# Two layers of routed experts: 33 slots of whole and quartered expert rows in place of 34 of whole and halved ones

## The chip, the cores and the metric

One core of a Trainium2 chip runs the whole program. The metric is the device time of one execution in microseconds (us). Engines are named as in the profile: PE is TensorE's matmuls, PEld its weight loads, DVE is VectorE, ACT is ScalarE, POOL is GpSimd, SP is SyncE. Rows are gathered and scattered by indirect DMAs that POOL issues.

## The reference

x has 8 x 256 = 2048 tokens of 512 values. Two layers follow each other, and each adds a routed feed-forward part to x. Cut to what matters here:

```python
# layer 0: each token takes two of 8 experts; an expert is a 512x512 matrix made from atoms
logits = clip(xt @ gate_w.T, -50, 50)
top_w, top_idx = top_k(logits, 2)
rw = softmax(top_w)
...                      # out = xt @ W.T + sum over the two of rw * (xt @ delta[expert])
x = x + layer0(...)      # xt is the attention's output

# layer 1
probs = softmax(x1 @ gate_w)
gate_score, gate_idx = top_k(probs, 2)
combine = onehot weights * alpha
h = gelu(x1 @ fc1_w[e] + fc1_b[e])
y = h @ fc2_w[e] + fc2_b[e]
out = sum over e of y[e] * combine[:, e]
```

So each layer has 2 x 2048 = 4096 pairs of token and expert, 512 for each expert on average. With the given inputs the experts hold 542, 416, 510, 556, 504, 526, 508 and 534 pairs in layer 0, and 542, 526, 490, 492, 520, 543, 510 and 473 in layer 1.

## The kernel before

**Slots.** A layer's pairs are laid into slots of 128 rows, 34 in each layer. A slot gathers its 128 token rows from DRAM (`fetched`, L682, an indirect DMA by POOL), turns them on PE (`turned`, L718 and L724, tile `pa`), multiplies them by an expert's weights (`multiplied`), scales each row by its routing weight and adds the rows to the result in DRAM by an accumulating indirect DMA (`added`, L729, POOL again).

**Plan.** `Plan` (L53) fixes at build time which expert a slot serves. *Full* slots serve one fixed expert; the first eight take the first 128 rows of each expert and only tokens of the first tiles, so that they can start early. The rest are *side* slots of two halves: the upper 64 rows go to a fixed expert (`plan.side`), the lower 64 to an expert that the routing finds at run time (`owners` reads it into registers). Layer 0 has 16 full and 18 side slots, layer 1 has 22 and 12. An expert's rows go in order of their rank to its first slot, its side halves, its further full slots and then to run-time halves. Rows that find no place are marked in `left`; if there are any, `run_rest` (L2095) routes and runs them in a slow branch. A token whose two rows fall into one slot is sent there too (`twice`, L514), because one accumulating DMA must not name a row twice.

**Routing.** `route` (L456) works out the slot and the row of each pair with a few dozen small DVE operations on 128 x 128 and 128 x 32 tiles, and `fill_slots` turns them into lists of tokens and weights with matmuls on one-hot tiles. `routing_constants` makes the plan's steps with iotas on POOL (L195).

**multiplied (L692).** A full slot runs four matmuls of 512 columns, one for each chunk of 128 of the contraction (the profile counts two instructions for each fp32 matmul). A side slot runs eight, on two column halves of the array in turn (L705), each half with its own 64 rows as the stationary operand and its own expert's weights as the moving one.

**slots0 (L1988)** is layer 0: one multiplication a slot, ACT scales the rows (L2029), and the adds of slot s go to one of two DRAM tensors, `sums_d[s % 2]`, which are added together later (`read`, L2152, loads `part` by SP at L2158). Weights of layer 1 are loaded meanwhile, one expert with each of the slots 8 to 23 (`load_first`, `load_second`).

**Between the layers** the adapters and the gate are folded on PE, `x1` is read, turned (L2165) and multiplied by the gate (`inner`, tile `px`, L2172, four column quarters), routed, and multiplied by the layer's matrix (`outer`, L2204), which fills PE until about 655 us.

**slots1 (L2263)** is layer 1. A full slot multiplies in turned form at once (L2299, tile `pu`); a side slot makes `ph`, copies it and turns it back (L718). ACT applies Gelu with the expert's bias, one instruction for each chunk and expert of the slot (L2325). The second multiplication gives `py`; DVE adds the second bias, once for each expert of the slot (L2341), and scales the rows (L2343). All adds go to `out`. The loop runs the first multiplication of slot s, then the second of slot s - 1, then Gelu of slot s, and turns the rows of slot s + 2; gathers run three or more slots ahead.

The program's order on the engines is fixed at build time. Before an add, POOL waits on semaphores for its input and for earlier adds to the same tensor.

Of the kernel before, what the change touches and what calls it, by code (L numbers as in the profile page):

```python
# [11 lines left out]
F32 = mybir.dt.float32  # L12
I32 = mybir.dt.int32
# [16 lines left out]
SCALE = 256.0**-0.5  # L30
EPS = 1e-6
E = 8
HR = P // 2
NREST = 2 * N // P + E - 1
NS = 4096
NSC = NS // P
# [16 lines left out]
class Plan:  # L53
# [5 lines left out]

    PAIRED, FULL = 128 * HR, 256 * HR

    def __init__(self, full, side, tiles):
        self.full = list(range(E)) + [e for e in range(E) for _ in range(full[e] - 1)]
        self.side = [e for e in range(E) for _ in range(side[e])]
        self.tiles = tiles
        self.F, self.D = len(self.full), len(self.side)
        self.n = self.F + self.D
        self.by_expert = []  # L70
        for e in range(E):
            t = P + HR * side[e]
            u = t + P * (full[e] - 1)
            early = self.FULL + P * e
            second = self.PAIRED + HR * (self.F + sum(side[:e])) - P
            whole = self.FULL + P * (E + sum(full[:e]) - e) - t
            first = HR * self.F - u
            self.by_expert.append((t, u, early + 1, second - early, whole - second, first - whole))


PLAN0 = Plan([2] * E, [2] * 6 + [3] * 2, 8)
PLAN1 = Plan([3] * 6 + [2] * 2, [1] * 6 + [3] * 2, 12)


@with_exitstack
def two_layer_kernel(ctx: ExitStack, tc: tile.TileContext, io: dict, out: bass.AP):
# [369 lines left out]
    def route(keep, pool, psum, consts, plan, sel, coef, tag, beside=None, skip=0, quads=False):  # L456
# [4 lines left out]
        pn, prk = ranks(pool, psum, consts, sel)  # L461
        have = pool.tile([P, E], F32, name="have")
        nc.vector.tensor_tensor(have, pn, fixed[:, 1, :], ALU.subtract)
        boff, bend = units(pool, keep, tag, consts, have, HR)
        nc.vector.scalar_tensor_tensor(
            boff, boff, float(HR), fixed[:, 5, :], ALU.mult, ALU.add
        )
        each = [P, NT, E]
        row = keep.tile(each, F32, name=f"row_{tag}")
# [23 lines left out]
        nc.vector.tensor_scalar(  # L493
            at_i, rows.rearrange("p r i -> p (r i)"), 1.0, None, ALU.subtract
        )
        is_full = pool.tile(both, F32, name="is_full")
        nc.vector.tensor_scalar(is_full, at_i, float(plan.FULL), None, ALU.is_ge)
        shift_i = pool.tile(both, I32, name="shift_i")
        nc.vector.tensor_scalar(shift_i, is_full, 6.0, None, ALU.add)
        mask_i = pool.tile(both, I32, name="mask_i")  # L500
        nc.vector.tensor_scalar(mask_i, is_full, float(HR), float(HR - 1), ALU.mult, ALU.add)
        second = pool.tile(both, F32, name="second")
        nc.vector.tensor_scalar(second, at_i, float(plan.PAIRED), None, ALU.is_ge)
        nc.vector.tensor_tensor(second, second, is_full, ALU.subtract)
        nc.vector.tensor_tensor(mask_i, at_i, mask_i, ALU.bitwise_and)
        rem = pool.tile(both, F32, name="rem")
        nc.vector.scalar_tensor_tensor(rem, second, float(HR), mask_i, ALU.mult, ALU.add)
        nc.vector.tensor_tensor(at_i, at_i, shift_i, ALU.arith_shift_right)
        nc.vector.tensor_scalar(at_i, at_i, 127, None, ALU.bitwise_and)
        slot = pool.tile(both, F32, name="slot")  # L510
        nc.vector.tensor_copy(slot, at_i)

        twice = pool.tile([P, NT], F32, name="twice")
        nc.vector.tensor_tensor(twice, slot[:, :NT], slot[:, NT:], ALU.is_equal)  # L514
        nc.vector.scalar_tensor_tensor(
            slot[:, :NT], twice, 128.0, slot[:, :NT], ALU.mult, ALU.add
        )
# [174 lines left out]
    def multiplied(py, xT, weights, experts):  # L692

        if len(experts) == 1:
            for k in range(KC):
                nc.tensor.matmul(  # L696
                    py,
                    xT[:, k, :],
                    of_expert(experts[0])(weights(k)),
                    start=(k == 0),  # L700
                    stop=(k == KC - 1),
                )
            return
        in_a_row(
            lambda k=k, h=h: nc.tensor.matmul(  # L705
                py[h * HR : (h + 1) * HR, :],
                xT[:, k, h * HR : (h + 1) * HR],
                of_expert(experts[h])(weights(k)),
                start=(k == 0),
                stop=(k == KC - 1),  # L710
            )
            for k in range(KC)
            for h in (1, 0)
        )

    def transposed(dst, src):
# [3 lines left out]
    def turned(pool, psum, xs, copy=nc.vector.tensor_copy):  # L720
        pa = psum.tile([P, KC, P], F32, name="pa")
        transposed(pa, xs)
        xsT = pool.tile([P, KC, P], F32, name="xsT")
        copy(xsT, pa)  # L724
        return xsT

    def added(sum_d, token, y):

# [1259 lines left out]
    def slots0(lists, owner_i, s0, end, plan=None):  # L1988


        with ExitStack() as ffn:
# [23 lines left out]
            for s in range(s0, end):  # L2015
                if plan and s < F:
                    experts = [plan.full[s]]
                else:
                    j = s - F
                    if j not in own:  # L2020
                        own.update(owners(owner_i[0], mybir.EngineType.PE, j))
                    experts = [own[j]] + ([plan.side[j]] if plan else [])
                if s + AHEAD_ROWS < end:
                    fetch(s + AHEAD_ROWS)
                py = ps_y.tile([P, D], F32, name="py")
                multiplied(py, xT.pop(s), lambda k: delta[k // HK][:, k % HK], experts)
                y = sx.tile([P, D], F32, name="y")
                _, token, weight = columns(lists, s)
                nc.scalar.mul(y, py, weight)  # L2029
                added(sums_d[s % 2], token, y)  # L2030
                if s + 2 < end:
                    xT[s + 2] = turn(s + 2)
                yield y
# [229 lines left out]
    def slots1(lists, owner_i, s0, end, plan=None):  # L2263

        with ExitStack() as moe:
# [14 lines left out]
            def experts(s, kind):  # L2280
                if plan and s < F:
                    return [plan.full[s]]
                j = s - F
                if (kind, j) not in own:
                    for key, engine in kinds.items():
                        have = owners(owner_i[0], engine, j)
                        own.update({(key, j): v for j, v in have.items()})
                return [own[kind, j]] + ([plan.side[j]] if plan else [])

            def turn(s):  # L2290
                return turned(sw, ps_a, xs.pop(s))
# [41 lines left out]
            def second_half(s, hs):  # L2333
# [7 lines left out]
                    nc.vector.tensor_tensor(y[rows], py[rows], of_expert(e, rows)(b2), ALU.add)  # L2341
                _, token, weight = columns(lists, s)
                nc.vector.tensor_scalar(y, y, weight, None, ALU.mult)  # L2343
                added(out, token, y)

            def fetch(s):
                rows_d = g_d[: plan.tiles * P, :] if plan and s < E else g_d
                xs[s] = fetched(sx, rows_d, columns(lists, s)[0])

            xs = {}  # L2350
            for s in range(s0, min(s0 + AHEAD_ROWS, end)):
                fetch(s)
            xT = {s: turn(s) for s in range(s0, min(s0 + 2, end))}
            hs = None
            for s in range(s0, end):
                had = first_half(s, xT.pop(s))
                if s + AHEAD_ROWS < end:
                    fetch(s + AHEAD_ROWS)
                if hs is not None:
                    second_half(s - 1, hs)  # L2360
                hs = middle(s, had)
                if s + 2 < end:
                    xT[s + 2] = turn(s + 2)
            second_half(end - 1, hs)

    found, owner_i, left_i, places = routed1
    slots1([(0, found)], [owner_i], 0, PLAN1.n, PLAN1)
# [88 lines left out]
```

## Time and profile before

| | |
|---|---|
| timed runs | 933.28, 938.00, 939.92 us; median 938.0 |
| profiled execution | 929.18 us, its span 927.5 us |
| PE busy | 885.9 us, 96% of the span, mean granted clock 0.991 |
| POOL busy | 358.4 us, 39% |
| layer 0's slots | 416 to 558 us, the 18 side slots from 484 |
| layer 1's slots | 657 to 918 us, the 12 side slots' from 817 |
| L729, adds to `out` | 34, mean 1586 ns each on POOL |
| L729, adds to `sums_d` | 34, means 1582 and 1617 ns |
| L682, gathers | 68, means 1027 to 1059 ns |

A profile's line for a group has the engine, the operation, the tiles (out<-in), the shapes and how often; idle time and what ended it stand in brackets. On POOL the time of a DMA_INDIRECT is that of its issue; the transfer goes on after it until the DMA lands.

### The profile page before, as it was taken

How to read it: one execution, taken by the hardware profiler on the slowest of the kernel's cores; microseconds unless marked ns; L12 is line 12 of the kernel's file. 1: busy time of each engine (PE TensorE's matmuls, PEld its weight loads, DVE VectorE, ACT ScalarE, POOL GpSimd, SP SyncE). 2: the span in 40 equal slices, each digit the busy share in tenths (PEclk: the TensorE clock that was granted, in tenths of full speed). 3: DMA queues.
4: the chain of work that ended last, by engine and by line, in shares of the span. 5: the costliest groups of instructions: out<-in, count | busy, mean ns of one | idle time of the engine just before them, and what ended most of it. 6: DMA issues, size and time to landing. Idle time of an engine off the chain costs nothing. (4 is left out here: it accounts for less than half of the span.)

```text
span 927.5 us, 13516 instructions
## 1 busy us (share of the span) xinstructions
PE 885.9 (96%) x4484; PEld 478.6 (52%) x4484; DVE 458.5 (49%) x1489; ACT 356.0 (38%) x952; POOL 358.4 (39%) x339
## 2 busy tenths in 40 slices
PE   6999999999999899999999998999999999999995
PEld 2654445555555455545443334454777777743332
DVE  4787879779777677682211113471122222222232
ACT  3676666566565556452222114311211111122231
POOL 3711355666656300154756740001233333333222
PEclk9899999999999999999999999999999999999998
DMA  7598494423522322185999858982544433433322
GB/s 203 195 313 294 141 311 123 126 36 93 166 51 49 103 69 92 50 290 118 184 329 311 184 81 259 346 325 78 194 71 75 73 69 69 69 69 66 49 30 30
DMA packets 73947, 134.05 MB, mean 145 GB/s; under 512 B 17277, under 2 KB 22909, under 8 KB 73744
## 3 DMA queue, kind: packets, MB, share of 16 engines
q0 software_dynamic: 25088, 43.68, 25.2%
q1 hardware_dynamic: 38208, 74.05, 23.1%
q10 hardware_dynamic: 10576, 15.39, 4.7%
q8 instruction: 38, 0.62, 0.3%
q14 instruction: 37, 0.30, 0.1%
HBM read 89.95 MB, written 52.04 MB: 153 GB/s over the span
## 5 line engine op out<-in xcount | busy, mean ns | idle before, releaser
L2341 DVE TENSOR_TENSOR y<-py,b 64x512 f32<-64x512 f32 (+1 forms) x46 | 31.7, 690 | 186.1 <-PE py L696 122.4
L682 POOL DMA_INDIRECT xs<-g_d,from_i_l x34 | 34.9, 1027 | 217.0 <-PE pa L718 131.8
L2325 ACT ACTIVATE hs<-pu,b 128x64 f32<-128x64 f32 (+1 forms) x184 | 46.2, 349 | 173.2 <-PE pu L2299 131.7
L1650 ACT ACTIVATE s<-s,mx,roots 128x384 f32<-128x384 f32 x128 | 89.8, 703 | 52.9 <-DVE mx L1648 52.0
L724 DVE COPY xsT<-pa 128x512 f32<-128x512 f32 x60 | 41.2, 688 | 126.6 <-PE pa L718 126.3
L2299 PE MATMUL pu<-xsT,w 128*128 128x128 f32 x704 | 82.3, 275 | 0.4 <-issue 0.4
L2299 PEld LDWEIGHTS pu<-xsT,w 128*128 128x128 f32 x704 | 80.3, 192 | 0.6 <-ACT g L2212 0.6
L696 PE MATMUL py<-w,hs 128*128 128x512 f32 x176 | 79.3, 593 | 0.0
L729 POOL DMA_INDIRECT out<-y,token_i_l x34 | 53.9, 1586 | 56.2 <-DVE y L2343 51.3
L1334 PE MATMUL pkv<-wkv,xb 128*128 128x512 f32 x128 | 67.5, 653 | 8.4 <-DMA wkv<-wqkvT 8.4
L1635 DVE CUSTOM_DVE_ANT_0 s<-ps,mask 128x384 f32<-128x384 f32 x128 | 67.6, 550 | 6.2 <-PE ps L1618 6.2
L1306 POOL DMA_INDIRECT delta_d<-entries,put_i x32 | 51.0, 1592 | 45.6 <-DMA delta_d<-entries,put_i 42.6
L705 PE MATMUL py<-delta,xsT 128*64 128x512 f32 (+1 forms) x288 | 65.5, 598 | 0.0
L1685 PE MATMUL po<-pT,kv 128*64 128x256 f32 x384 | 57.5, 389 | 7.9 <-ACT pT L1675 4.9
L1673 PEld LDWEIGHTS pp<-ident,s 128*128 128x128 f32 x384 | 42.1, 141 | 37.0 <-issue 23.9
L1267 PE MATMUL pq<-wq,xb 128*128 128x512 f32 x128 | 60.3, 595 | 0.7 <-DVE lg L1715 0.7
L798 PE MATMUL ph<-woT,oT 128*128 128x512 f32 x128 | 59.1, 594 | 0.0
L696 PE MATMUL py<-delta,xsT 128*128 128x512 f32 x128 | 58.5, 596 | 0.0
L2204 PE MATMUL pc<-wc,x1T 128*128 128x512 f32 x128 | 58.5, 596 | 0.0
L1673 PE MATMUL pp<-ident,s 128*128 128x128 f32 x384 | 56.3, 280 | 2.3 <-DVE pT L1675 1.3
L1618 PE MATMUL ps<-KT,QT 64*128 64x384 f32 x256 | 53.7, 520 | 0.4 <-DVE KT L1592 0.4
L729 POOL DMA_INDIRECT sums_d<-y,token_i_l x26 | 41.1, 1582 | 32.1 <-ACT y L2029 13.8
(430 smaller groups left out, 1486.3 us busy)
## 6 DMA issues: line engine op xcount, KB each, us to landing
delta_d<-spread SPq DMA_DIRECT2D x16, 512.0 KB, 6.0
raw<-delta_d SPq DMA_DIRECT2D x16, 512.0 KB, 4.6
w<-fc_w SPq DMA_DIRECT2D x8, 1024.0 KB, 15.2
part<-sums_d SPq DMA_DIRECT2D x32, 256.0 KB, 5.0
w<-fc_w SPq DMA_DIRECT2D x8, 768.0 KB, 10.3
xb<-xT SPq DMA_DIRECT2D x5, 1024.0 KB, 6.1
sums_d<-zero SPq DMA_DIRECT2D x18, 256.0 KB, 5.2
kv_new<-kvt ACTq DMA_DIRECT2D x16, 256.0 KB, 3.1
```

Of the source, the lines that this page charges most:

```text
L696: nc.tensor.matmul(py, xT[:, k, :], of_expert(experts[0])(weights(k)), start=(k == 0), stop=(k == KC - 1),)
L705: lambda k=k, h=h: nc.tensor.matmul(py[h * HR : (h + 1) * HR, :], xT[:, k, h * HR : (h + 1) * HR], of_expert(experts[h])(weights(k)), star ...
L729: nc.gpsimd.indirect_dma_start(out=sum_d, out_offset=bass.IndirectOffsetOnAxis(ap=token, axis=0), in_=y, in_offset=None, bounds_check=sum_ ...
L798: nc.tensor.matmul(ph, oTs[i // 2][:, k, (i % 2) * P : (i % 2 + 1) * P], woT[:, k, :], start=(k == 0), stop=(k == KC - 1),)
L1267: nc.tensor.matmul(pq, xcols[:, k, :], wq[:, k, :], start=(k == 0), stop=(k == KC - 1))
L1334: nc.tensor.matmul(pkv, xb[:, k, cols], wkv[:, k, :], start=(k == 0), stop=(k == KC - 1),)
L1635: nc.vector.tensor_tensor_reduce(out=s, in0=ps[:, r, :WU], in1=mask[:, t, :], scale=1.0, scalar=NEG, op0=ALU.add, op1=ALU.max, accum_out=m ...
L1650: nc.scalar.activation(ss[r], ss[r], AF.Exp, bias=mx[:, r : r + 1], scale=root[:, r : r + 1], accum_out=sm[:, r : r + 1],)
L1673: nc.tensor.transpose(pp[:, c, :], part, ident)
L1685: nc.tensor.matmul(po[r * HD : (r + 1) * HD].rearrange("p m q -> p (m q)"), kvs[t + c][:, v0 + r * HD : v0 + (r + 1) * HD], pT[:, 3 * r + ...
L2204: nc.tensor.matmul(pc, x1T[:, k, i * P : (i + 1) * P], wc[:, k, :], start=False, stop=(k == KC - 1),)
L2299: nc.tensor.matmul(pu[:, c, :], w1[:, k, plan.full[s], c * P : (c + 1) * P], xsT[:, k, :], start=(k == 0), stop=(k == KC - 1),)
```

## The change

Both layers get the same plan of 33 slots: 24 full slots (three for each expert) and 9 slots of four quarters of 32 rows. Three quarters of such a slot belong to fixed experts, the lowest to one found at run time. Experts 3 and 4 take their quarters after their further full slots, the others before. `route` works out the places in quarters, and `twice` now compares halves of a slot, so a token may stand in both halves of one slot. For that reason a quarter slot is added in two DMAs of 64 rows: in layer 0 the lower half to `sums_d[0]` and the upper to `sums_d[1]`, in layer 1 both to `out`. The upper half's tokens are copied once to the lower partitions (`upper_tokens`). Layer 1 runs its last full slot, F - 1 = 23, after the quarter slots.

```diff
-HR = P // 2
+QR = P // 4
...
+    PARTS = P // QR
+    def __init__(self, whole, quarters, last, tiles):
+        self.full = list(range(E)) + [e for e in range(E) for _ in range(whole)]
+        side = [e for e in range(E) for _ in range(quarters[e])]
         self.tiles = tiles
-        self.F, self.D = len(self.full), len(self.side)
+        self.F, self.D = len(self.full), len(side) // (self.PARTS - 1)
         self.n = self.F + self.D
+        self.fixed = [side[j :: self.D] for j in range(self.D)]
...
-PLAN0 = Plan([2] * E, [2] * 6 + [3] * 2, 8)
-PLAN1 = Plan([3] * 6 + [2] * 2, [1] * 6 + [3] * 2, 12)
+PLAN0 = Plan(2, [3] * 3 + [4] * 3 + [3] * 2, (3, 4), 8)
+PLAN1 = Plan(2, [3] * 3 + [4] * 3 + [3] * 2, (3, 4), 12)
...
-        boff, bend = units(pool, keep, tag, consts, have, HR)
+        boff, bend = units(pool, keep, tag, consts, have, QR)
...
+        at = pool.tile(both, F32, name="at_f")
+        nc.vector.tensor_copy(at, at_i)
+        in_row = pool.tile(both, F32, name="in_row")
...
+        nc.vector.tensor_scalar(at_i, at_i, 6, None, ALU.arith_shift_right)
+        twice = pool.tile([P, NT], F32, name="twice")
+        nc.vector.tensor_tensor(twice, at_i[:, :NT], at_i[:, NT:], ALU.is_equal)
...
+        n = P // len(experts)
         in_a_row(
             lambda k=k, h=h: nc.tensor.matmul(
-                py[h * HR : (h + 1) * HR, :],
-                xT[:, k, h * HR : (h + 1) * HR],
+                py[h * n : (h + 1) * n, :],
+                xT[:, k, h * n : (h + 1) * n],
                 of_expert(experts[h])(weights(k)),
...
-            for h in (1, 0)
+            for h in reversed(range(len(experts)))
...
+    def upper_tokens(pool, plan, lists):
+        first, have = lists[-1]
+        upper = pool.tile([P // 2, plan.D], I32, name="upper", bufs=1)
+        nc.vector.tensor_copy(upper, have[1][P // 2 :, plan.F - first :])
+        return upper
+    def added_in_halves(sums, tokens, y):
+        for h, token in enumerate(tokens):
+            added(sums[h], token, y[h * P // 2 : (h + 1) * P // 2])
...
-                    experts = [own[j]] + ([plan.side[j]] if plan else [])
+                    experts = [own[j]] + (plan.fixed[j] if plan else [])
...
+                if plan and s >= F:
+                    added_in_halves(
+                        sums_d, (token[: P // 2], upper[:, s - F : s - F + 1]), y
+                    )
+                else:
+                    added(sums_d[s % 2], token, y)
...
+                if plan and s >= F:
+                    added_in_halves(
+                        (out, out), (token[: P // 2], upper[0][:, s - F : s - F + 1]), y
+                    )
+                else:
+                    added(out, token, y)
...
+            seq = list(range(s0, end))
+            if plan:
+                seq.append(seq.pop(F - 1))
...
+            second_half(seq[-1], hs)
```

## The prediction

> **What bounds the kernel now.** I read the busy totals first, then the table of busy time by stage (columns: stretch, its length, then busy us and instruction count of PE, PEld, DVE, ACT and POOL, then the granted TensorE clock, the DMA share and GB/s).
>
> ```profile
> PE 885.9 (96%) x4484; PEld 478.6 (52%) x4484; DVE 458.5 (49%) x1489; ACT 356.0 (38%) x952; POOL 358.4 (39%) x339
> ...
> 484.00:558.00 74.00, 73.84 (x353) 25.87 (x352) 11.76 (x17) 13.85 (x28) 43.77 (x32) 1.00 0.85 194
> 558.00:575.00 17.00, 14.69 (x76) 8.75 (x76) 6.23 (x20) 8.19 (x17) 1.56 (x1) 1.00 0.84 243
> 700.00:824.00 124.00, 124.00 (x713) 88.36 (x712) 30.89 (x48) 18.89 (x65) 43.55 (x33) 1.00 0.42 73
> 824.00:918.00 94.00, 92.90 (x458) 35.49 (x456) 28.87 (x46) 27.46 (x107) 25.10 (x18) 1.00 0.30 45
> 918.00:927.50 9.50, 0.00 (x0) 0.00 (x0) 1.49 (x3) 0.00 (x0) 1.55 (x1) 0.69 0.27 39
> ```
>
> TensorE is full in every slot stage, at full clock: 484 to 558 are layer 0's half slots, 700 to 824 layer 1's full slots, 824 to 918 its half slots. The exceptions are 17 us between the layers (2.3 idle) and 9.5 us of tail. So a slot costs its TensorE time, as long as the scatter-adds behind it keep up. The PE and POOL timelines give both (start, length, engine, line; in brackets the idle time before and what ended it):
>
> ```profile
> 806.02 3.60 PE L696 MATMUL py<-w,hs 128*128 128x512 f32 x8
> 809.45 0.60 PE L718 MATMUL pa<-ident,xs 128*128 128x128 f32 x4
> ...
> 833.56 3.65 PE L705 MATMUL ph<-w,xsT 128*64 128x512 f32 x16
> 837.04 3.60 PE L705 MATMUL py<-w,hs 128*64 128x512 f32 x16
> ...
> 575.43 1.08 PE L2172 MATMUL px<-x1T,aTg 128*32 128x128 f32 x32 [0.39 <-ACT x1T L2166]
> ```
>
> ```profile
> 192.78 1.55 POOL L1306 DMA_INDIRECT delta_d<-entries,put_i  x1 [1.83 <-DMA delta_d<-entries,put_i]
> 196.09 1.55 POOL L1306 DMA_INDIRECT delta_d<-entries,put_i  x1 [1.76 <-DMA delta_d<-entries,put_i]
> ...
> 493.69 1.59 POOL L729 DMA_INDIRECT sums_d<-y,token_i_l  x1 [1.80 <-DMA sums_d<-y,token_i_l]
> 498.08 1.59 POOL L729 DMA_INDIRECT sums_d<-y,token_i_l  x1 [1.45 <-DMA sums_d<-y,token_i_l]
> ...
> 914.81 1.56 POOL L729 DMA_INDIRECT out<-y,token_i_l  x1 [6.05 <-DVE y L2343]
> 920.89 1.55 POOL L729 DMA_INDIRECT out<-y,token_i_l  x1 [4.53 <-DVEq L2097]
> ```
>
> Last, the DMA view (name, issuer, count, median us from issue to landing):
>
> ```profile
> delta_d<-entries,put_i POOLq DMA_INDIRECT x7, 3.1
> ...
> out<-y,token_i_l POOLq DMA_INDIRECT x13, 4.9
> ```
>
> The reader is to see that an add waits for the landing of the earlier add to the same tensor. In layer 1 no such wait shows, because adds stand 7.4 to 8.0 us apart and land in 4.9.
>
> **TensorE's side.** From the starts of successive slots, a full slot takes 3.87 us in layer 0 and 7.45 in layer 1, a half slot 4.17 and 8.04. A half slot issues twice the instructions (16 for 8), two abreast, in the same 3.6 us. A quarter slot issues 32, four abreast. The px row has this form already: 32 products in 1.08 us, starts of successive groups of four 0.109 us apart, against 0.107 us for one full product of 128 columns. So four streams cost what one does, and I price a quarter slot as a half slot.
>
> Layer 0 goes from 16 full and 18 half slots to 24 and 9: 8 x 3.87 - 9 x 4.17 = **-6.6 us** (PE ends at 551.3 instead of 557.8). Layer 1 goes from 22 and 12 to 24 and 9: 2 x 7.45 - 3 x 8.04 = -9.2, and with the full slot now last, the final transposes and the 0.7 us wait for Gelu go: PE ends at 907.4 instead of 917.6, **-10.2 us**.
>
> The Trainium skill, "TensorE: Matmul & The Clock Gate", section "Measured speedup vs the span model", has three column tiles gain only 2.38 times. By an estimate from that page, at 79% of the gain each 3.5 us block of a quarter slot would take 4.4, and the 27 blocks (9 and 18) would add 25 us; the px row shows no such loss.
>
> **Small parts, priced at nothing.** Gelu has 16 instructions instead of 8 per slot: 8 take 1.75 us now, so at most 3.6; they end near 844.9 where their product starts at 845.08, and that product needs only the first chunk then. Four bias adds instead of two make y later by 2 x 0.69 = 1.4 us; DVE is free 5 us of 8. Routing has 16 small DVE operations for 11 (0.17 to 0.25 us each, so +1.2 at most): in layer 1 it ends at 630 while PE has outer products until 655; in layer 0 it lies beside the early slots, which run until 452. Without that cover each would cost its 1.2. Ten constant iotas (0.98 us) become 18: +0.8 on POOL at 438, where gathers run slots ahead. The copy of the upper tokens is one short DVE operation. Capacity: the inputs fill 9 of 9 free quarters in layer 0 and 8 of 9 in layer 1, so nothing is left for the slow branch.
>
> **POOL's side, the unknown.** A quarter slot has two adds of 64 rows instead of one of 128. Let x be their time from issue to landing. Nothing here has 64 rows. A 128-row add takes 1.56 to issue; with 32-byte rows it lands at 3.1 (1.5 after), with 2 KB rows at 4.7 to 4.9 (1.7 more for the data). Bounds: all of it halves, 2.4; nothing does, 4.9. I halve the data (0.85) and keep the 1.5. For the issue, a 128-row gather takes 1.04; the 0.52 that adding costs more is work on rows, so I halve it, and give up half of half the rest: 1.56 - 0.26 - 0.26 = 1.04. So **x = 3.4**, nearer the adds than the halved bound.
>
> By the Trainium skill, "DMA: Bandwidth & Descriptors", section "Anatomy of one DMA — SWDGE (gpsimd) path", a DMA has 2.0 us fixed plus bytes over 436 GB/s. Half the bytes would then save an estimated 0.3 us, x = 4.6, and by the sums below the change would lose about 23 us. The rows above differ by 1.7 us for the bytes where the page has 0.6, so I go by the rows.
>
> After a landing, the next add starts 0.27 us later where that is its only wait (the delta_d pair: landed 3.04 after issue, next at 3.31) and 0.78 later where it waits for its input too (488.93 landed 8.37 later, next at 498.08).
>
> *Layer 1* has one tensor. The lower add, the upper add after its landing, the next slot's lower add after that: 2x + 0.27 + 0.78 = 7.85 us a slot, against 8.04 of PE. It just fits (the first lower add starts at 844.4). The break-even of that pair is x = 3.5; beyond it every slot adds 2x - 7.0 over eight slots. The tail: the last quarter slot's product ends at 903.85, four bias adds, the scaling and the dispatch take 3.65, lower add 907.5, upper 911.2, and the full slot's add, ready at about 909, waits until 915.35. It lands 4.7 later and the program ends 1.9 after that, as now: 922.0 against 927.5, **-5.5 us**. So half of PE's gain goes into waiting.
>
> *Layer 0* has two tensors, lower to one and upper to the other, each x + 0.78 = 4.18 a slot against 4.17 of PE. But the adds are already late at this point: during the weight loads they land in 7 to 8 us, and the add of slot 23 starts at 520.94 now, 2.9 us late. It stays there, since its predecessors wait for landings and for POOL, not for PE. Half slots then drain the delay at 3.26 us of POOL each; quarter slots can't. From slot 23: slot 24 at 524.2, three more gathers, slot 26 at 533.6, six more slots at 4.18, last lower add 558.7, upper 560.1, landing 563.5; it is 558.90 + 4.84 = 563.7 now. So x1 is read no earlier. PE, 6.5 us early, does its gate folding sooner and then waits: the first px moves from 575.43 to some 574.4. From there PE is full to the end of the stage, so layer 0 keeps **-1 us**.
>
> **Sum.** -5.5 - 1.0 = -6.5 us against the profiled execution's 929.18 (span 927.5 and 1.7 around it). That one lies below all three timed runs (933.28 to 939.92), so I take the difference to their median: 938.0 - 6.5 = **931.5 us**.
>
> **The rivals**, all by the same two chains.
> 1. *The adds keep up* (x up to 3.1). At x = 3.0 the last add of layer 0 lands near 560.2 (-4.5 with the 1 us above), layer 1 gives -6.3: -10.8, 927. At 2.4 all of PE's 6.6 counts and layer 1 gives -7.5: 924. For it: packets of half the rows; against it: an issue time that does not depend on the row's length.
> 2. *The adds become the bound: slower.* Place: POOL's queue in the quarter slots, each add behind the landing of the one before. Price: layer 1 pays 16 us and its tail 2 more per us of x above 3.5, layer 0 some 8. It decides from x = 3.7, where the sum is zero. At 3.9 it is +6, at 4.25 (64 rows spread over half the DMA engines, so the data part does not shrink) +14, at 4.9 +31. For it: the two rates of 7.85 and 4.18 have no room.
> 3. *Quarters don't run four abreast.* Three at a time: 27 blocks x 1.1 = +30, less 6.5: 961. Against it: the px row. The same chance holds a token left over: the slow branch routes again (some 30 us, as from 600 to 630) and runs a slot, +40.
>
> **How the numbers follow.** My forecast, x of 3.15 to 3.65, has 0.42; rival 1 0.23; rival 2 0.30, 0.08 of it within 1%; rival 3 0.05. One per cent, 9.4 us, is about what a measurement of this kernel can tell from no change. Faster by more: rival 1, 0.23. Within: 0.42 + 0.08 = 0.50. Slower: 0.22 + 0.05 = 0.27. The likeliest case alone is 929 to 938. The range goes from 923 (x = 2.4, and a us for the run) to 947 (x = 4.05), which leaves some 0.2 above.
>
> **What would show it.** Right: quarter slots 8.04 us apart on PE with 32 instructions in 3.6 us; PE's last product near 907; 64-row adds that take about 1.05 to issue and land after 3.4; the final add at least 7 us after PE's end; the first read of sums_d still near 561. Wrong: a landing above 3.7 or below 3.1, PE idle inside quarter slots, POOL idle between quarter adds, a second pass through L650's branch.

## The result, and the profile after

The changed kernel takes 940.13 us (median of 20 runs, 934.87 to 945.41), and the kernel before, run beside it, 934.98 us (20 runs, 928.41 to 939.92). The ratio is 1.0063 with a 95% interval of 1.0040 to 1.0085: the change costs 0.6%. The profiled execution took 938.09 us, its span is 936.4 us, against 927.5 before. PE's busy time did fall, by 13 us. Totals and stages of the changed kernel (columns as in the prediction):

```profile
PE 872.8 (93%) x4800; PEld 480.6 (51%) x4800; DVE 468.4 (50%) x1511; ACT 362.0 (39%) x1005; POOL 380.3 (41%) x369
...
552.00:560.00 8.00, 6.06 (x32) 3.72 (x32) 0.00 (x0) 3.81 (x7) 4.61 (x5) 1.00 0.46 55
560.00:573.00 13.00, 0.00 (x0) 0.00 (x0) 1.79 (x10) 0.00 (x0) 3.89 (x3) 0.58 0.66 161
573.00:590.00 17.00, 15.90 (x98) 9.22 (x99) 7.46 (x16) 7.18 (x16) 0.00 (x0) 0.82 0.83 296
...
824.00:917.20 93.20, 93.16 (x747) 38.38 (x745) 40.02 (x61) 34.71 (x163) 33.56 (x25) 1.00 0.30 48
917.20:936.40 19.20, 0.00 (x0) 0.00 (x0) 1.18 (x2) 0.00 (x0) 4.59 (x4) 0.59 0.24 31
```

Two stretches are new. Between the layers PE does nothing for 13 us and then works at a lowered clock; before, the 17 us between the layers had 2.3 us of idle time. And behind PE's last product stand 19.2 us instead of 9.9. The slots themselves are as full as before.

The PE timeline of the quarter slots in layer 1, and POOL's timeline of the last adds there:

```profile
858.59 3.64 PE L722 MATMUL ph<-w,xsT 128*32 128x512 f32 x32
862.05 3.62 PE L722 MATMUL py<-w,hs 128*32 128x512 f32 x32
...
866.62 3.64 PE L722 MATMUL ph<-w,xsT 128*32 128x512 f32 x32
```

```profile
915.98 1.41 POOL L758 DMA_INDIRECT out<-y,upper  x1 [2.63 <-DMA out<-y,token_i_l]
920.40 1.41 POOL L758 DMA_INDIRECT out<-y,token_i_l  x1 [3.01 <-DMA out<-y,upper]
923.74 1.41 POOL L758 DMA_INDIRECT out<-y,upper  x1 [1.93 <-DMA out<-y,token_i_l]
928.12 1.57 POOL L758 DMA_INDIRECT out<-y,token_i_l  x1 [2.96 <-DMA out<-y,upper]
```

A quarter slot takes 8.03 us of PE (858.59 to 866.62). But behind the first pair the adds wait for the landing of the one before, as the brackets say, and no longer for their input. From the first lower add (853.99) to the last (920.40) eight slots take 66.4 us, 8.30 each. PE was done at 917.16. The chain that ended last shows the landing itself (start, length, what):

```profile
899.48 3.57 DMA out<-y,upper
...
907.50 3.69 DMA out<-y,upper
```

Layer 0's adds, and what stands between the layers (timelines of the changed kernel, POOL first):

```profile
523.91 1.47 POOL L758 DMA_INDIRECT sums_d<-y,token_i_l  x1 [0.30 <-issue]
526.46 1.43 POOL L758 DMA_INDIRECT sums_d<-y,upper  x1 [1.08 <-issue]
528.19 1.06 POOL L698 DMA_INDIRECT xs<-h_d,from_i_l  x1 [0.30 <-DMA sums_d<-y,token_i_l]
...
557.76 1.41 POOL L758 DMA_INDIRECT sums_d<-y,token_i_l  x1 [1.23 <-DMA sums_d<-y,token_i_l]
559.65 1.41 POOL L758 DMA_INDIRECT sums_d<-y,upper  x1 [0.49 <-DMA sums_d<-y,upper]
562.23 1.41 POOL L758 DMA_INDIRECT sums_d<-y,token_i_l  x1 [1.16 <-DMA sums_d<-y,token_i_l]
563.94 1.41 POOL L758 DMA_INDIRECT sums_d<-y,upper  x1 [0.30 <-issue]
```

```profile
566.09 25.73 SPq L2194 DMA_DIRECT2D part<-sums_d  x32
571.21 0.69 DVE L2195 TENSOR_TENSOR part<-part,part 128x512 f32<-128x512 f32 x1 [25.86 <-DMA part<-sums_d]
571.82 1.15 DVE L1973 TENSOR_SCALAR pick<-pbg,use 128x8 f32<-128x8 f32 x8
573.03 2.07 PE L1988 MATMUL pga<-pick,an 128*128 128x256 f32 x4 [13.74 <-DVE pick L1973]
```

PE's last product of layer 0 ends at 551.62. The lower adds lag it by 10.6 us at the end, so SP reads x1 from 566.09, 4.7 us later than before the change. And DVE now has the first addition of x1 rows *ahead of* the eight `pick` operations of the gate's folding: PE's `pga`, which needs `pick` and no x1, waits 13.74 us for rows that it does not use. In the kernel before, `pick` came first:

```profile
562.75 1.16 DVE L1944 TENSOR_SCALAR pick<-pbg,use 128x8 f32<-128x8 f32 x8 [1.74 <-PE pbg L1940]
567.31 0.69 DVE L2159 TENSOR_TENSOR part<-part,part 128x512 f32<-128x512 f32 x1 [3.40 <-DMA part<-sums_d]
```

The program builder, the software that fixes each engine's order, had put them the other way round for the changed kernel.

The span's 8.9 us, taken apart by stage (worked out from the two timelines):

| stage | before | after | difference |
|---|---|---|---|
| up to layer 0's first product | 416.79 | 417.24 | +0.45 |
| layer 0's products | 141.05 | 134.38 | -6.67 |
| PE's end there to the first read of x1 | 3.59 | 14.47 | +10.88 |
| first read of x1 to the first add on `out` | 108.94 | 113.85 | +4.91 |
| first add on `out` to PE's last product | 247.23 | 237.22 | -10.01 |
| PE's last product to the end | 9.89 | 19.21 | +9.32 |

PE won 16.7 us, as planned, and what stands behind PE took 25.1.

### The profile page after: what moved, and what is told of

It is laid out like the page before. It is cut to its first block, busy times and chain, and to the rows that moved or that the text cites. A ratio compares the mean times of both kernels' runs of the same rounds, so it can differ in the third digit from the quotient of the medians.

```text
span 936.4 us, 14190 instructions
## 1 busy us (share of the span) xinstructions
PE 872.8 (93%) x4800; PEld 480.6 (51%) x4800; DVE 468.4 (50%) x1511; ACT 362.0 (39%) x1005; POOL 380.3 (41%) x369
## 3 DMA queue, kind: packets, MB, share of 16 engines
q1 hardware_dynamic: 38208, 74.05, 22.8%
## 5 line engine op out<-in xcount | busy, mean ns | idle before, releaser
L2377 DVE TENSOR_TENSOR y<-py,b 32x512 f32<-32x512 f32 (+1 forms) x60 | 41.3, 689 | 166.5 <-PE py L712 127.7
L2361 ACT ACTIVATE hs<-pu,b 128x32 f32<-128x32 f32 (+1 forms) x240 | 54.1, 349 | 169.6 <-PE pu L2335 138.6
L2335 PE MATMUL pu<-xsT,w 128*128 128x128 f32 x768 | 89.8, 275 | 0.4 <-issue 0.4
L2335 PEld LDWEIGHTS pu<-xsT,w 128*128 128x128 f32 x768 | 87.6, 192 | 0.6 <-ACT g L2248 0.6
L712 PE MATMUL py<-delta,xsT 128*128 128x512 f32 x192 | 87.3, 595 | 0.0
L712 PE MATMUL py<-w,hs 128*128 128x512 f32 x192 | 86.6, 593 | 0.0
L758 POOL DMA_INDIRECT out<-y,token_i_l x33 | 51.0, 1547 | 38.3 <-DMA out<-y,upper 19.6
L1258 POOL DMA_INDIRECT kv<-kv_new,idx_new x32 | 33.7, 1053 | 48.1 <-DMA kv_new<-kvt 29.4
L712 PEld LDWEIGHTS py<-w,hs 128*128 128x128 f32 x192 | 34.6, 190 | 36.1 <-issue 30.8
```

The source lines that it names most:

```text
L712: nc.tensor.matmul(py, xT[:, k, :], of_expert(experts[0])(weights(k)), start=(k == 0), stop=(k == KC - 1),)
L758: nc.gpsimd.indirect_dma_start(out=sum_d, out_offset=bass.IndirectOffsetOnAxis(ap=token, axis=0), in_=y, in_offset=None, bounds_check=sum_ ...
L2335: nc.tensor.matmul(pu[:, c, :], w1[:, k, plan.full[s], c * P : (c + 1) * P], xsT[:, k, :], start=(k == 0), stop=(k == KC - 1),)
L2361: nc.scalar.activation(hs[:, k, j * n : (j + 1) * n], pu[:, k, j * n : (j + 1) * n], AF.Gelu, bias=b1[:, slice(col, col + 1) if isinstance ...
```

## The experiments

Each ratio is against the kernel before, run on the same chip. The runs came in four groups, A to D, on different chips. The changed kernel itself had 1.0063 in the comparison above and 1.0139 in group D; it has no run in A, B or C. So ratios are compared within a group, and across groups I compare lengths of stages. The changed kernel was profiled twice: layer 0's products took 134.38 us both times, the stretch from the first read of x1 to the first add on `out` 113.85 and 113.50, the tail 19.21 and 19.53. The stretch from PE's end in layer 0 to the first read repeats less well, 14.47 and 15.29 here, and 15.48 and 13.24 in another kernel with two profiles. What stands ahead of layer 0's first product scatters most, 417.24 and 427.44 us, so a part of any difference in time between two kernels is scatter from there.

**1. Layer 1 alone (group A).** Theory: two adds a slot, one behind the other on the same tensor, eat what PE wins.

```diff
-PLAN0 = Plan(2, [3] * 3 + [4] * 3 + [3] * 2, (3, 4), 8)
+PLAN0 = HalfPlan([2] * E, [2] * 6 + [3] * 2, 8)   # layer 0's plan of before
```

> Quarters in layer 1 alone; layer 0 keeps its halves. Theory 2 (two adds per slot on one tensor): layer 1's 10.0 us on PE are handed back at its end by the chain of adds on the output, whose last one comes some 11 us after PE's end instead of 3.3, and by 1.5 us more behind it; the ratio is about 0.999 (-0.7 us), the first add on the output falls near 670.4 as before the change, and a lower add follows the last every 8.3 us against 8.04 for PE's slot. Rival (the disturbance of layer 0 is carried on): the late end of the adds in layer 1 is a consequence of its late start, so with layer 0 as before it keeps the 5.5 us that the prediction worked out: ratio 0.994.

Measured: 0.9990 (0.9970 to 1.0010). Layer 1's stage from its first add to PE's end is 236.1 us long (247.2 before), its tail 19.6 (9.9). The first add came at 676.30 and not near 670.4, but this execution reached layer 0 4.4 us later and its read of x1 at 565.85. Theory 2 holds: with layer 0 as it was, the tail takes back 9.7 of the 11.2 us that PE wins in layer 1, and the ratio can't be told from 1.

**2. The adds without the quarters (group A).** The kernel before, only with its half slots' adds split.

```diff
-                added(out, token, y)
+                if plan and s >= F:
+                    added_in_halves((out, out), (token[: P // 2], upper...), y)
+                else:
+                    added(out, token, y)
```

> The kernel before, with its 34 slots of halves and its PE work unchanged, but the add of each of the half slots (18 in layer 0, 12 in layer 1) split into two of 64 rows. Theory 2: a pair of adds takes 4.4 to 4.5 us per slot in layer 0 (2 tensors in turn) against PE's 4.17, and 8.3 us in layer 1 (one tensor) against 8.04: with no gain on PE the adds cost about 5 us at the end of layer 0, the order of the x1 addition on DVE (which flips here too) some 3 to 7 us more, and about 8 us at the end of layer 1; ratio 1.015 to 1.022. Rival (the adds are no limit; the quarter products or the routing cost the time): the split adds hide under PE and the ratio is 1.00 to 1.003.

Measured: 1.0390 (1.0354 to 1.0426), more than expected. Split adds alone cost 37 us where PE saves nothing, though with 30 split slots instead of 18. Layer 1's tail is 19.2 us. In layer 0 the 18 pairs cost more than I reckoned: POOL's own issue, a gather and two adds (1.06 + 1.44 + 1.41 and three gaps of 0.30), is 4.8 us a slot against PE's 4.17, so the gathers come late and PE waits for rows. Layer 0's products take 144.7 us, and x1 is read 22.8 us after PE's end.

**3. One of the two adds left out (group A).** The kernel leaves out the upper 64 rows of every quarter slot, and it also has `pick` pinned as in experiment 5.

```diff
-                    added_in_halves((out, out), (token[: P // 2], upper...), y)
+                    added(out, token[: P // 2], y[: P // 2])     # layer 0 likewise
```

> The changed kernel with the order pinned as in the first of these kernels, and only the lower 64 rows of each quarter slot added; the upper adds are left out (their rows are missing from the sums). Theory 2: one 64-row add per slot keeps up with PE in both layers; the last one is issued within 1 us of the row it adds, layer 0's first px comes 5 to 7 us earlier than before the change (near 569), and layer 1 keeps its 10 us on PE with the 9.9 us tail of before: ratio 0.981 to 0.985. Rival (PE's quarter products, the routing or the clock bound it): no more than 3 us below the pinned kernel with both adds, ratio above 0.993.

Measured: 0.9841 (0.9816 to 0.9867), as theory 2 has it; with the pin and both adds it is 1.0055 in the same group. x1 is read 4.9 us after PE's end, px follows 12.7 us later, layer 1's tail is 11.7 us (9.9 expected). With one add a slot the change wins 15 us, so the quarter products, the routing and the Gelus cost next to nothing. This run leaves out half of the rows along with the second add; experiment 2, with all rows and two adds, is its counterpart.

**4. Quarter slots spread among full ones (groups B and C).** In layer 1, slots 0 to 7, then a full and a quarter slot in turn, then seven full ones.

```diff
-                seq.append(seq.pop(F - 1))
+                seq = list(range(E)) + [t for j in range(plan.D) for t in (E + j, F + j)] + list(range(E + plan.D, F))
```

With halves in layer 0:

> Halves in layer 0 as before the change; quarters in layer 1, alternating with full slots. Theory 2: layer 1's 10 us on PE are kept, since the chain of adds on the output keeps up; layer 0 is as before; ratio 0.988 to 0.991. Rival: as the kernel with quarters in layer 1 alone, 0.999.

Measured: 0.9941 (0.9921 to 0.9961). The end of POOL's timeline of this kernel:

```profile
912.76 1.55 POOL L810 DMA_INDIRECT out<-y,token_i_l  x1 [5.26 <-DVE y L2431]
918.13 1.55 POOL L810 DMA_INDIRECT out<-y,token_i_l  x1 [3.81 <-DMA out<-y,token_i_l]
```

The add before the last waits for its input again (DVE's `y`), and the tail is 9.9 us as before the change. The mechanism is the expected one, but 5.5 us came where 8 to 11 were expected. Part of the gap is PE's: a full and a quarter slot in turn take 15.81 us, 0.32 more than the sum of the two apart (7.45 + 8.04), nine times. Of the versions that add all rows, this is the one clearly faster than the kernel before.

With quarters in both layers, and the folding first (see 6):

> As the kernel with the folding first and the reads in order, and layer 1's quarter slots alternating with full ones. Theory 2: 5 to 8 us less than that kernel (the earlier pair gave 0.5%), ratio 0.995 to 1.000, last add 3 to 4 us behind PE's end. Rival: no more than 2 us less.

Measured: 1.0002 (0.9979 to 1.0025), against 1.0078 unspread in the same group. The tail went from 20.2 to 11.5 us.

**5. `pick` pinned ahead of the x1 addition (group A).** Now to layer 0. Theory: the builder's order on DVE did it.

```diff
-            x1 = {i: read(i) for quad in quads for i in quad}
+            with tc.issue_after(picked[-1].ins):
+                x1 = {i: read(i) for quad in quads for i in quad}
```

> The changed kernel with one order pinned: on DVE the first x1 addition is issued only behind the eight pick operations of the gate's folding. Theory 1 (order): in the changed kernel the folding waited on DVE for the landing of the last adds, because the x1 addition stood ahead of it. With the order pinned, PE's 13.7 us pause between the layers shrinks to the 3 to 5 us it had before the change, the clock stays at 1.00 there, and the first product of layer 1's routing (px) comes at about 579 us instead of 586.4: from the x1 addition at 571.2 plus the 8.1 us that lay between this addition and px before the change. That is 7 us less than the changed kernel, about 0.999 of the kernel before. Rival (late landing): the x1 rows come late whatever the order, and px can't start before them; then the pin is worth at most 2 us and the ratio stays at 1.004 to 1.008.

Measured: 1.0055 (1.0028 to 1.0082), the rival's figure. `pga` came at once, but PE then waited 10.5 us at the first transposes of x1 rows, which stand ahead of the folding's second half in PE's own order:

```profile
581.09 0.87 PE L2205 MATMUL pt<-ident,part 128*128 128x128 f32 x3 [10.54 <-issue]
```

So the 7 us of the theory didn't come. A part did: px followed the first read by 17.0 us (20.3 in the changed kernel, 14.0 before it), and the first add on `out` followed it by 110.5 us instead of 113.85. In this profile the read itself came later, 16.3 us after PE's end instead of 14.5, so that 1.5 of the 3.3 us are left in it.

**6. The whole folding first (groups B, C and D).** The x1 additions behind the folding's last operation on DVE, the x1 transposes behind its last on PE.

```diff
+            with tc.issue_after(ended["DVE"].ins):
+                x1 = {i: read(i) for quad in quads for i in quad}
...
+            with tc.issue_after(ended["PE"].ins), tc.issue_after(ended["ACT"].ins):
                 for k in range(KC):
                     nc.tensor.transpose(pt[:, k, :], ...)
```

> The changed kernel with the whole folding of the gate (its last reduction and additions on DVE, its last transposes on PE, its last copy on ACT) issued ahead of everything that waits for the x1 rows; the pin of pick alone only moved the wait from DVE to PE, where the first transposes of x1 stand ahead of the folding's second half. Theory 1 (order, now on PE and DVE): the first px follows the fifth x1 addition by about 2 us, near 579 to 581 on the changed kernel's clock instead of 586.4; 5 to 7 us are won, ratio 0.999 to 1.001. Rival (late landing and a lower granted clock): PE then idles even longer ahead of the x1 rows, the clock falls as before, and no more than 2 us are won, ratio 1.004 to 1.007.

Measured: 1.0118 (1.0088 to 1.0149). px did come early, 12.3 us behind the first read, yet the first add on `out` came 115.9 us behind it (113.85 in the changed kernel). The pin had a side effect: the builder also moved SP's reads, many rows of one tensor first, and the fifth row was complete only at 585.98. So this run and the next, which has layer 1 spread besides, say little on the order; their difference bears out experiment 4 once more.

> As the kernel with the whole folding first, and in layer 1 the nine quarter slots alternate with full ones (slots 0 to 7, then full and quarter slots in pairs, then seven full ones) instead of standing together near the end. Nothing is left out. Theory 2 (two adds per slot): three adds now have two slots of PE time, 15.8 to 16 us, against about 13 us for the chain; no lateness is built up, the last add is issued 3 to 4 us behind PE's end instead of 11, and 8 to 9 us are won on the kernel with the whole folding first. Rival (the lateness of layer 1 comes from its late start or from POOL's queue as a whole): at most 2 us are won.

Measured: 1.0066 (1.0045 to 1.0087), the tail 11.7 us instead of 19.6. Then with the reads held in their old order:

> The changed kernel with the whole folding of the gate ahead of the x1 rows, as before, and SP's reads of the x1 rows kept in the pairs of the changed kernel (in the earlier version the builder had also moved the reads: it read many rows of the one tensor first, and the fifth row was complete only at 586). Theory 1 (order): first px about 12 us behind the first read, no gap between the x1 additions, 3 to 5 us less than the changed kernel, ratio 1.001 to 1.003. Rival (the granted clock): the folding was what kept PE at work behind the wait; now PE stands idle right ahead of the x1 transposes, which come in pieces, the clock falls to 0.5 for them and for the first products of layer 1, and at most 1 us is won: 1.005 to 1.008.

Measured: 1.0078 (1.0050 to 1.0106). By the letter that is the rival's figure, but the changed kernel's 1.0063 is from another comparison. So both ran side by side in group D:

> The changed kernel once more, as the standard for the others of this group: 1.004 to 1.009 of the kernel before.

> The kernel with the folding of the gate first and the reads of x1 in order, on the same chip as the changed kernel. Theory 1 (order): 3 us or more less than the changed kernel (its first add of layer 1 came 113.9 us behind the first read of x1, with the folding first 111.2). Rival (the read's start alone decides): within 1 us of the changed kernel.

Measured: 1.0139 (1.0102 to 1.0176) for the changed kernel and 1.0084 (1.0049 to 1.0119) with the folding first. The intervals overlap a little; the medians, 949.33 and 943.85, are 5.5 us apart. In the profiles the stretch from the first read of x1 to the first add on `out` is 113.3 to 113.9 us in the three with quarters in layer 0 and the builder's order, and 111.2 to 111.6 in the three with the folding first, the reads in order and nothing else changed up to there. Some 2.2 us of the order's price are shown; the rest of the 5.5 lies within the scatter. The late read remains: 13.2 to 15.5 us after PE's end in all of them.

**7. PE kept at work (group C).** The clock fell in the changed kernel and with the folding first. Does that cost time?

```diff
+            def keep_busy(n):
+                with tc.issue_after(ended["PE"].ins):
+                    for _ in range(n):
+                        ended["PE"] = nc.tensor.matmul(spare, ident, GB[:, 0, :], start=True, stop=True)
+            keep_busy(8)
```

> As the last one, with eleven products of 128x512 added on PE whose result nobody reads: eight between the end of the folding and the first x1 transposes, one behind each of the first three rows' transposes. Clock theory: PE isn't idle long enough for the clock to fall, the granted clock is 1.00 from 560 to 600, and the first add of layer 1 comes 109 us behind the first read of x1 (as before the change: 561.4 to 670.4) instead of 114: 4 to 6 us less than without these products, ratio 1.000 to 1.002. Rival (the clock costs nothing, since PE waits for rows anyway): the same time as without them, or up to 3 us more.

Measured: 1.0071 (1.0044 to 1.0098) against 1.0078 without. Two stretches of the stage table, first without, then with the extra products:

```profile
560.00:573.00 13.00, 5.97 (x26) 2.89 (x25) 1.61 (x6) 3.05 (x7) 4.71 (x4) 0.87 0.62 125
573.00:590.00 17.00, 14.63 (x117) 8.91 (x116) 7.62 (x13) 5.43 (x11) 0.00 (x0) 0.70 0.99 354
```

```profile
560.00:573.00 13.00, 11.54 (x38) 5.32 (x38) 2.31 (x7) 3.06 (x7) 3.81 (x3) 1.00 0.71 162
573.00:590.00 17.00, 16.53 (x138) 9.59 (x136) 7.83 (x13) 7.03 (x14) 0.00 (x0) 1.00 1.05 386
```

The clock stays at 1.00, and from the first read to the first add on `out` it is 110.9 us instead of 111.2. So the 4 to 6 us of the clock theory didn't come. But the timelines don't show that the clock is free. Here are the first px and the transposes behind it, without and then with the extra products, and ACT's copy behind the second px of the latter:

```profile
579.39 1.93 PE L2213 MATMUL px<-x1T,aTg 128*32 128x128 f32 x32 [0.68 <-ACT x1T L2207]
581.25 1.11 PE L2206 MATMUL pt<-ident,part 128*128 128x128 f32 x4
```

```profile
579.30 1.08 PE L2213 MATMUL px<-x1T,aTg 128*32 128x128 f32 x32 [0.24 <-ACT x1T L2207]
580.31 0.66 PE L2206 MATMUL pt<-ident,part 128*128 128x128 f32 x4
...
593.56 0.59 ACT L2207 COPY x1T<-pt 128x512 f32<-128x512 f32 x1 [3.22 <-DMA out<-part]
```

Counted from the first read, the second px came at 18.7 us with the extra products and at 20.6 without them; then ACT's wait of 3.22 us put the third at 28.1 against 27.2. Later, the kernel without them has 3.4 us more at half clock (610.6 to 614.1), and its products between the fourth px and the end of `outer` take 62.7 us instead of 61.5. What the lowered clock alone costs stays unsettled; these rows speak for 1 to 3 us.

**8. The upper adds put aside (group D).** What makes the x1 rows late?

```diff
-                        sums_d, (token[: P // 2], upper[:, s - F : s - F + 1]), y
+                        (sums_d[s % 2], aside_d), (token[: P // 2], upper[:, s - F : s - F + 1]), y
```

> As the kernel with the folding first, but in layer 0 the upper adds of the quarter slots go to a third tensor that nobody reads (their rows are missing from the sums), and the lower ones alternate between the two tensors; POOL issues as many adds and fetches as before. If the landing of one add before the next is what makes the x1 rows late (theory 2 in layer 0), each tensor now has two slots' time, 8.3 us, for an add of about 4.4; only POOL's own 4.83 us per slot stand against PE's 4.17 while it still fetches, and the last lower add is issued within 2 to 4 us of PE's last product of the layer instead of 10.6; the reads of x1 start 6 to 8 us earlier, ratio 0.999 to 1.002. If POOL's issue is the limit, the adds stay late and the time is that of the kernel with the folding first.

Measured: 1.0008 (0.9976 to 1.0041), against 1.0084 with the folding first in the same group. The lower adds wait for no landing any more:

```profile
553.92 1.41 POOL L761 DMA_INDIRECT aside_d<-y,upper  x1 [1.22 <-DMA aside_d<-y,upper]
555.63 1.41 POOL L761 DMA_INDIRECT sums_d<-y,token_i_l  x1 [0.30 <-issue]
557.85 1.41 POOL L761 DMA_INDIRECT aside_d<-y,upper  x1 [0.80 <-DMA aside_d<-y,upper]
```

The last one is issued 5.1 us after PE's end instead of the 9.4 with the folding first in this group, and x1 is read 9.9 us after PE's end instead of 13.2. The lateness shrank less than expected (2 to 4 us were to be left), since the upper adds still wait for one another, and the lower ones stand behind them on POOL. So the landings on the two tensors that x1 is read from make some 4 of the 9.4 us. How the rest divides between POOL's issue and the chain of the upper adds isn't shown.

**9. Layer 0 alone (group D).**

```diff
-PLAN1 = Plan(2, [3] * 3 + [4] * 3 + [3] * 2, (3, 4), 12)
+PLAN1 = HalfPlan([3] * 6 + [2] * 2, [1] * 6 + [3] * 2, 12)   # layer 1's plan of before
```

> Quarters in layer 0 alone, layer 1 with halves as before the change. If the two layers' changes simply add up, this costs what the whole change costs less layer 1's part (1.0063 less 0.999): ratio 1.006 to 1.009, first add of layer 1 near 680. Rival (layer 1's late end is caused by layer 0's lateness, or the other way round): under 1.004 or over 1.011.

Measured: 1.0117 (1.0080 to 1.0154). That is above the figures expected and, by the letter, on the rival's side, but the whole change is as far up on this chip, 1.0139; the first add on `out` came at 684.44, from a layer 0 that began 4.8 us later than in the profile before. Layer 0's stages are those of the changed kernel (read 15.1 us after PE's end, the first add on `out` 113.3 us after that), and the tail is 10.8 us, near the 9.9 of before. The two layers add up within the intervals: layer 0 carries the loss, layer 1 comes out even.

**10. Spread in both layers (group B).** Layer 0's quarter slots alternate as well; the moved reads of 6 are in here too.

```diff
-                    added(sums_d[s % 2], token, y)
+                    added(to[0], token, y)
+                    to = to[::-1]          # `to` starts as sums_d: strict turn
```

> Quarters in both layers, alternating with full slots in both, the whole folding first; layer 0's adds go to its two tensors in strict turn. Theory 2: layer 0 keeps most of its 6 us on PE too, since three adds in two slots (8.0 us of PE) need about 7.2 us of each tensor's chain; 4 to 6 us less than with layer 1 alone spread, ratio 0.983 to 0.987. Rival (POOL's issue becomes the bound): two fetches and three adds with their gaps take POOL 2 x 1.06 + 1.59 + 2 x 1.41 + 5 x 0.30 = 8.03 us per pair of slots against PE's 8.04, so that every wait on it is added up; then nothing is won on the kernel with layer 1 alone spread, or up to 5 us are lost.

Measured: 1.0049 (1.0023 to 1.0074), beside 1.0066 with layer 1 alone spread. The rival is right: layer 0's products take 141.8 us instead of 134.4, with PE waiting up to 1.76 us for gathered rows. Neither of the two places tried for the quarter slots has room on POOL for a second add in layer 0.

## Why the prediction failed

The forecast was 931.5 us, 6.5 us less than before; the change costs 5 to 6 us (8.9 between the two profiles). By its steps:

- **PE's price of a quarter slot: right.** 32 instructions in 3.62 to 3.64 us, 8.03 us a slot in layer 1. Layer 0's products are 6.67 us shorter (6.6 predicted), layer 1's stage 10.0 (10.2). The Trainium skill's figure of 2.38 times for three column tiles ("TensorE: Matmul & The Clock Gate", "Measured speedup vs the span model") would mean a loss; these rows, with four column tiles, show none.
- **The small parts at nothing: right, to within 2 us.** With one add left out the change wins 15 of the 16.7 us that PE saved.
- **x, the landing of a 64-row add: mis-sized.** 3.57 to 3.69 us in the rows shown, and not 3.4. The issue is where it went wrong: 1.41 us against the 1.04 that I took, so half the rows saved a tenth of the 1.56 to 1.59 and not a third. With 3.65 the prediction's own formula, 2x + 1.05, gives 8.35 us a slot in layer 1; the trace has 8.30. The estimate from the skill's "DMA: Bandwidth & Descriptors" ("Anatomy of one DMA — SWDGE (gpsimd) path"), 4.6, was farther off.
- **Layer 1's end: right in kind, too small.** The tail grew by 9.3 us where 4.7 were predicted. Of the missing 4.6, 3.1 are the last lower add, 3.24 us after PE's end instead of 0.1: slots of 8.30 against 8.03, and the first lower add. Another 1.6 are a longer end behind the final add (last section).
- **Layer 0's last adds: too early.** From slot 26 on the forecast had 4.18 us a slot; it was 4.4 to 4.5, and one slot of 5.7, so the last lower add came at 562.23 instead of 558.7 and the first read at 566.09 instead of 561. So x1 was read 4.7 us later than before the change, where the sum had it unchanged.
- **"PE, 6.5 us early, does its gate folding sooner and then waits": the step that failed.** The steps above have a wrong size; this one has a wrong mechanism. It took the order of the kernel before as given. The builder set it anew, with an x1 addition ahead of `pick`, and the folding came *after* the wait. The first px came at 586.38, not at 574.4: 4.7 us of the 12 are the later read, 6.3 are px following the read by 20.3 us instead of 14.0, and the last 1.0 is the gain that layer 0 was to keep. Of the 6.3 us 4.9 are left at the first add on `out`. Undoing the order by hand gave back 2.2 of them (the whole folding first) or 3.3 (`pick` alone, in one profile); the rest isn't shown to be the order's.
- **Put together.** From layer 0's first product on, the forecast was -6.5 us and the two profiles differ by +8.4. By the prediction's own prices, x of 3.65 instead of 3.4 is worth some 4.9 of these 14.9 us. Layer 0's read is late by another 2.2, the stretch from the read to the first add on `out` is longer by 4.9, for which the sum had no term, layer 0's gain of 1.0 didn't come, and the end behind the final add took 1.7; 0.2 are PE's.
- **The rivals.** Rival 2 is what came about, in its place, with x at its threshold of 3.7, where it was priced at zero: what tipped it over is for the larger part layer 0, where the last adds came later than x alone makes them and the folding waited. So its kind was foreseen; that x alone would decide was not borne out.

Open: the stretch behind the first read stays 1 to 2 us longer with the folding first (111.2 to 111.6) than with halves in layer 0 (108.9 to 110.5). In the timelines about 1 us stands ahead of the fourth px and 1.1 in the outer products behind it, both where the granted clock is lowered for a while in the kernels with the folding first and at 1.00 in those with halves; no run isolates it. And spreading with halves in layer 0 won 5.5 us in time (3.6 to 7.4 by the interval), 7.5 in the profile from layer 0's first product on.

## What to carry to other kernels

Here a slot cost the longer of its engine's time and of the chain of accumulating DMAs behind it; where each waits for the landing of the one before, price the chain by issue plus landing, and let units with two adds alternate with units with one. Halving such a DMA's rows took a tenth off its issue and a quarter off its landing here, so two halves cost 1.5 times the whole in the chain and 1.8 times on POOL. When an engine is said to "go on sooner", look up what stands ahead of that work in the order of *every* engine that feeds it, in the changed program and not in the old one.

## What the runs showed of the hardware

- In the changed kernel an accumulating indirect DMA of 64 rows of 2 KB takes POOL 1.41 to 1.47 us to issue, one of 128 rows mostly 1.57 to 1.63; in layer 1 the upper halves on the chain that ended last landed 3.57 to 3.72 us after the start of the issue, and for 128 rows the median before the change is 4.7 to 4.9.
- Four column quarters of the array, with different weights each, run without loss: 32 instructions in 3.64 us where eight full ones take 3.60.
- In the changed kernel PE stood idle from 559.3; the granted clock fell to 0.5 at about 562.2, 2.9 us later, and came back at about 579.3, 6.2 us after PE was at work again. In the profiles that have them, the lowered stretches between the layers last 3.4, 6.8, 10.2, 13.7, 17.1 or 20.5 us, multiples of 3.41. The Trainium skill ("TensorE: Matmul & The Clock Gate", "What's actually happening") has at least one window of about 3.4 us, idle or busy, for either way. The fall comes near one window of idle time, the return near two of work.
- The stretch from the last add's issue to the end is 6.6 us before the change and 8.0 to 8.3 in the changed kernel and in most others with quarters in layer 0, but 6.4 to 6.9 in the three with halves there; with quarters in layer 0 it was also 6.4 once (spread in both layers), 6.6 once (lower adds only) and 7.5 once (layer 0 alone). The last landing isn't what differs: SP's wait for it ends 4.6 us after the issue in the changed kernel and 4.7 before. The 1.7 us are two of POOL's own closing instructions, 1.38 and 4.98 us long instead of 0.53 and 4.13. Why they take longer is open.
